# Constant first states for three scans in four: a selective scan whose carried states move to the first column, on one Trainium2 core

## The chip, the cores and the metric

The kernel runs on one core of a Trainium2 chip (trn2), as one launch. The metric is the device time of that launch in microseconds: the median of several executions of the same program. Beside it stands one profiled execution, from which every view of the trace is taken.

## The reference

Two layers follow each other on an input `x` of 4 images, 128 channels, 128 x 128 pixels, all fp32. The first is a selective state space model over the 16384 pixels of an image, taken as a sequence:

```
h1 = relu(xf @ mlp_w1.T + mlp_b1);  xm = h1 @ mlp_w2.T + mlp_b2
x_in, z = split(xm @ in_proj_w.T)
u = silu(causal_conv4(x_in) + conv_b)
dt, Bm, Cm = split(u @ x_proj_w.T)
delta = softplus(dt @ dt_proj_w.T + dt_proj_b);  A = -exp(A_log)
h = h * exp(delta * A) + delta * u * Bm      # per step: 256 channels x 16 states
y = sum over the states of h * Cm
out = ((y + u * D) * silu(z)) @ out_proj_w.T, group norm, silu, + x
```

The second layer weighs four spectral filters by a softmax of a pooled projection, and applies them in the Fourier domain. The change touches the line with `h` alone.

## The kernel before

The program has two blocks. `block0` is the first layer, up to about 6385 us of the span; `block1` is the second. Each engine runs its own queue in order.

`block0` cuts the sequence of an image into 32 **chunks** of 512 steps (`T`), so there are 128 chunks, counted `k`. The 256 channels x 16 states of a chunk are 4096 independent recurrences, 32 tiles of 128 partitions (32 channels x 4 states): a half `j` (2), a round `r` (4) and a place `p` (4). The function `place(r, p)` says which group of 32 channels stands at place `p` of round `r`. One `(j, r)` is a **unit** (8 in a chunk, unit 0 to unit 7), and its two pairs of places (0, 1 and 2, 3) are two **slots** `n`; a chunk is 16 slots (`NP`). What each engine does in a slot is an order written by hand: lists of (slot, phase, function), and within a slot the phases in the fixed order of the last loop of `block0`.

For one unit this happens:

- `dbu` (L370, GpSimd) makes du*B for places 1 to 3 in the tile `hb`, two slots ahead, from `rdu` and `rB`, which DMAs have spread over the partitions. For place 0 TensorE makes it in `b0` (L390), from `bt`.
- `exps` (L400, ScalarE) makes exp(delta*A) into `da`, one to three slots ahead. Places 1 to 3 lie in PSUM, one buffer each.
- `scans` (L419, VectorE) runs h = da*h + b along the 512 steps. Its first state `init` is 0 in the first chunk of an image; else it is one column of the tile `last` (shown as `st`), the last state of the same tile in chunk `k - 1`.
- h*C: for some places VectorE (L421), in place over `da`, for the others GpSimd (L426), from the tile `h`. `by_vector` says which: places 2 and 3 on VectorE, 0 and 1 on GpSimd as one instruction over two places, and some exceptions by the chunk's parity and by `norming(k)`. A chunk is norming when it is chunk 2 to 17 of image 1, 2 or 3, all counted from 0 (48 chunks: `k % 32` from 2 to 17); there the group norm of the image before runs beside the scans. The other 80 chunks are called plain here.
- The last state of each place is copied to `last` by ScalarE, one column after a VectorE product (L422), one or two columns after a GpSimd place (L561, in the next slot's phase `late`).
- `sums` (L440, TensorE) adds up h*C over the states.

Beside the scans, each chunk has its projections, convolution, SiLUs (L244, L247), softplus (L283) and `du` = delta*u on GpSimd (L319) for the next chunk, on slots that `pre` lists. ScalarE loads a table (`ACT_TABLE_LOAD`) when it goes from Exp to SiLU or softplus and back.

Of the kernel before, what the change touches and what calls it, by code (L numbers as in the profile page):

```python
# [26 lines left out]
F32 = mybir.dt.float32  # L27
AF = mybir.ActivationFunctionType
ALU = mybir.AluOpType
# [4 lines left out]
P = 128  # L34
T = 512
# [11 lines left out]
def kernel(ctx: ExitStack, tc: tile.TileContext, a: dict, out: bass.AP):  # L47
# [106 lines left out]
    spec = [dpool.tile([H, C, 2, WF], F32, tag=f"spec_{b}", name=f"spec_{b}") for b in range(EARLY)]  # L154
    shared = SimpleNamespace(**{k: v for k, v in locals().items() if k not in ("ctx", "tc")})
    block0(tc, shared)
    block1(tc, shared)


def block0(tc, s):  # L160
    nc, B, NCH, NH, NS, NG, ND, R, NX, KC, HALO, C, L, NF, DI = (
        s.nc, s.B, s.NCH, s.NH, s.NS, s.NG, s.ND, s.R, s.NX, s.KC, s.HALO, s.C, s.L, s.NF, s.DI,
    )
    NT, TH, HP = T // P, T // 2, P // 2
    with ExitStack() as ctx:
        def pool(name, bufs, **kw):
            return ctx.enter_context(tc.tile_pool(name=name, bufs=bufs, **kw))
# [4 lines left out]
        tiny = pool("tiny", 2)  # L172
# [13 lines left out]
        st = {}  # L186
        stats, outs = s.stats, s.outs

        def pre(k):
# [3 lines left out]
            b, i = divmod(k, NCH)  # L193
            d = st[k] = {}
# [127 lines left out]
            def rep_load(j):  # L322
# [9 lines left out]
                (NP - 2, "pe", z_mm), (NP - 1, "act", z_act), (NP + 2, "act", z_silu), (3, "pe", xd_mm), (4, "act", xd_act), (5, "pe", dt_mm), (5, "pe", xd_turn),  # L332
                (5 if k else 7, "act", bc_load), (6, "act", dt_act), (7, "act", xd_turn_act), (7, "pool", du_pool),
                (8, "pe", partial(du_turn, 0)), (9, "act", partial(rep_load, 0)),
                (8, "pool", partial(bt_act, 0, 0, 1)), (9, "act", partial(bt_act, 0, 1, 5)),
                (10, "act", partial(bt_act, 0, 5, 8)), (11, "pe", partial(du_turn, 1)),
                (11, "pool", partial(bt_act, 1, 0, 1)), (12, "act", partial(bt_act, 1, 1, 2)),
# [7 lines left out]
        def norming(k):  # L345

            return k >= NCH and 2 <= k % NCH < 2 + NCH // 2

        def place(r, p):


            return (p - r) % ND

        def by_vector(k, j, r, p):

            if norming(k):
                return p > 1 and (k % 2 == 1 or (j, r, p) != (1, 2, 2))
            return p > 1 or (k % 2 == 1 and (j, r, p) == (1, 2, 1))

        def dbu(u):  # L360

            k, r = divmod(u, NH * NG)
            j, r = divmod(r, NG)
            d = st[k]
            hb = d["hb", j, r] = hpool.tile([P, ND, T], F32, tag="hb", name=f"hb_{k}_{j}_{r}")
            p = 1
            while p < NG:
                m = place(r, p)
                n = min(NG - p, ND - m)
                nc.gpsimd.tensor_tensor(  # L370
                    hb[:, p : p + n, :], d["du", j][:, m : m + n, :], d["B"][:, p - 1 : p - 1 + n, :], ALU.mult
                )
                p += n

        def pair(n):

            k, r = divmod(n, NP)
            u, p = divmod(r, ND // 2)
            j, r = divmod(u, NG)
            return k, j, r, 2 * p  # L380

        def dbu_turn(n):

            k, j, r, p = pair(n)
            d = st[k]
            if p == 0:
                b = d["b0"] = psd.tile([P, T], F32, tag="b0", name=f"b0_{k}_{j}_{r}")
                for t in range(NT):
                    src = d["bt"][:, t, j * ND + place(r, 0), :, :].rearrange("p s d -> p (s d)")
                    nc.tensor.transpose(b[:, t * P : (t + 1) * P], src, s.ident)  # L390

        def exps(n, qs):

            k, j, r, p = pair(n)
            d = st[k]
            for q in qs:
                m = place(r, p + q)
                c = (j * NG + p + q) * ND + m
                da = (psd if p + q else p2).tile([P, T], F32, tag=f"da{p + q}", name=f"da{p + q}_{k}_{j}_{r}")
                nc.scalar.activation(da, d["delta", j][:, m, :], AF.Exp, scale=s.amat[:, c : c + 1])  # L400
                d["da", j, r, p + q] = da

        def scans(n):


            k, j, r, p = pair(n)
            d = st[k]
            hb = d["hb", j, r]
            das = [d.pop(("da", j, r, p + q)) for q in range(2)]
            dve = [q for q in range(2) if by_vector(k, j, r, p + q)]  # L410
            pool = [q for q in range(2) if q not in dve]
            last = d["last", j, r, p] = tiny.tile([P, 2], F32, tag=f"st{j}_{r}_{p}", name=f"st_{k}_{j}_{r}_{p}")
            if pool:
                h = p2.tile([P, 2, T], F32, tag="h", name=f"h_{k}_{j}_{r}_{p}", bufs=3)
            for q in range(2):
                b = hb[:, p + q, :] if p + q else d.pop("b0")
                init = 0.0 if k % NCH == 0 else st[k - 1]["last", j, r, p][:, q : q + 1]
                o = das[q] if q in dve else h[:, q, :]
                nc.vector.tensor_tensor_scan(o, das[q], b, init, ALU.mult, ALU.add)  # L419
            for q in dve:  # L420
                nc.vector.tensor_tensor(hb[:, p + q, :], das[q], d["C"][:, p + q, :], ALU.mult)  # L421
                nc.scalar.copy(last[:, q : q + 1], das[q][:, T - 1 : T])  # L422
            if pool:
                q = slice(pool[0], pool[-1] + 1)
                ps = slice(p + pool[0], p + pool[-1] + 1)
                nc.gpsimd.tensor_tensor(hb[:, ps, :], h[:, q, :], d["C"][:, ps, :], ALU.mult)  # L426
                todo[n + 1, "late"].append(partial(nc.scalar.copy, last[:, q], h[:, q, T - 1]))

        def sums(u):

# [81 lines left out]
        todo = defaultdict(list)  # L512
        for k in range(n_chunks):
            for at, phase, f in pre(k) + post(k):
                todo[at + (k - 1) * NP, phase].append(f)
# [30 lines left out]
        for n in range(n_chunks * NP):  # L546
            if n % 2 == 0:
                todo[n - 3, "early"].append(partial(exps, n, (0,)))
            todo[n - 1, "exps"].append(partial(exps, n, (1,) if n % 2 == 0 else (0, 1)))
            todo[n - 1, "turn"].append(partial(dbu_turn, n))  # L550
            todo[n, "scans"].append(partial(scans, n))
            if n % 2 == 0:
                todo[n - 2, "dbu"].append(partial(dbu, n // 2))
            else:
                todo[n + 2, "sums"].append(partial(sums, n // 2))
        slots = [n for n, _ in todo]
        with tc.manual_schedule():
            for n in range(min(slots), max(slots) + 1):
                for phase in ("turn", "sums", "pe", "exps", "late", "act", "pool", "dbu", "early", "gate", "scans", "dve", "end"):
                    for f in todo[n, phase]:  # L560
                        f()  # L561

# [509 lines left out]
```

## Time and profile before

| | |
|---|---|
| Median of 3 executions | 7099.01 us (7092.6 to 7100.89) |
| Profiled execution: time, span | 7100.83 us, 7099.1 us |
| Mean granted TensorE clock | 0.926 |
| Busy in the span | DVE (VectorE) 6843.7 us, POOL (GpSimd) 6807.6, ACT (ScalarE) 6144.4, PE (TensorE) 5656.9 |
| Scans (L419) | 4096, most 1.255 to 1.27 us each |
| h*C on VectorE, on GpSimd | 2064 instructions of one place; 984 of two places and 64 of one |

The profile is of one execution. A row of a group reads: line, engine, operation, tile written and tiles read, shapes, count, then busy time in us and mean ns of one, then the engine's idle time just before them and what ended it. A row of waits reads: who waited for whom, us in total, times, longest. A timeline row starts with its start in us and its length; equal neighbours are merged, and what stands in brackets is the engine's idle time before it. On VectorE, ScalarE and GpSimd an instruction starts some 0.04 to 0.1 us before the one ahead of it has ended, so the time that one takes from its engine is the distance of the starts, a little less than its length.

### The profile page before, as it was taken

How to read it: one execution, taken by the hardware profiler on the slowest of the kernel's cores; microseconds unless marked ns; L12 is line 12 of the kernel's file. 1: busy time of each engine (PE TensorE's matmuls, PEld its weight loads, DVE VectorE, ACT ScalarE, POOL GpSimd, SP SyncE). 2: the span in 40 equal slices, each digit the busy share in tenths (PEclk: the TensorE clock that was granted, in tenths of full speed). 3: DMA queues.
4: the chain of work that ended last, by engine and by line, in shares of the span. 5: the costliest groups of instructions: out<-in, count | busy, mean ns of one | idle time of the engine just before them, and what ended most of it. 6: DMA issues, size and time to landing. Idle time of an engine off the chain costs nothing.

```text
span 7099.1 us, 95554 instructions
## 1 busy us (share of the span) xinstructions
PE 5656.9 (80%) x28724; PEld 2700.3 (38%) x28724; DVE 6843.7 (96%) x7901; ACT 6144.4 (87%) x13836; POOL 6807.6 (96%) x3010
## 2 busy tenths in 40 slices
PE   6777777787777778787787778887778787877999
PEld 2333333333333333333333333333333333327888
DVE  6999999999999999999999999999999999997877
ACT  6888888888888888888989888898988989878886
POOL 6999999999999999999999999999999999997887
PEclk8988898888989989999999999999999999989999
DMA  6667667667787767777777777777878777768865
GB/s 141 160 153 164 159 149 165 160 150 175 179 196 181 188 169 167 181 181 179 192 193 196 189 174 177 174 184 172 200 188 200 191 170 178 169 143 293 273 218 190
DMA packets 759513, 1288.54 MB, mean 182 GB/s; under 512 B 81728, under 2 KB 192848, under 8 KB 758992
## 3 DMA queue, kind: packets, MB, share of 16 engines
q1 hardware_dynamic: 758848, 1282.16, 72.5%
q8 instruction: 226, 3.70, 0.2%
q14 instruction: 295, 2.42, 0.1%
q10 hardware_dynamic: 144, 0.26, 0.0%
HBM read 1025.52 MB, written 256.58 MB: 181 GB/s over the span
## 4 chain that ended last, share of the span: by engine, by line
ACT 30%; DVE 24%; POOL 18%; PE 10%; issue 10%; DMA 7%; SPq 1%; DVEq 0%; ACTq 0%; POOLq 0%
DVE da L419 12%; ACT da L400 12%; POOL hb L370 10%; POOL hb L426 7%; DVE h L419 7%; ACT L400 3%; DVE hb L421 3%; DMA rdelta<-dd 2%; ACT bt L313 2%; PE px L892 2%; DMA rdu<-dd 2%; ACT L247 2%; ACT L283 1%; ACT delta L283 1%; PE y L440 1%
## 5 line engine op out<-in xcount | busy, mean ns | idle before, releaser
L370 POOL TENSOR_TENSOR hb<-rdu,rB 128x1536 f32<-128x1536 f32 (+2 forms) x1536 | 3612.4, 2370 | 41.6 <-DMA rdelta<-dd 21.2
L400 ACT ACTIVATE da<-rdelta,amat 128x512 f32<-128x512 f32 x4096 | 2792.3, 699 | 123.3 <-DVE h L419 119.3
L426 POOL TENSOR_TENSOR hb<-h,rC 128x1024 f32<-128x1024 f32 (+1 forms) x1048 | 2411.1, 2302 | 89.3 <-DVE h L419 76.6
L419 DVE TENSOR_TENSOR_SCAN da<-da,st,hb 128x512 f32<-128x512 f32 x2000 | 2449.3, 1268 | 38.0 <-ACT da L400 27.1
L421 DVE TENSOR_TENSOR hb<-da,rC 128x512 f32<-128x512 f32 x2064 | 1309.7, 673 | 2.2
L419 DVE TENSOR_TENSOR_SCAN h<-da,st,b 128x512 f32<-128x512 f32 x992 | 1258.7, 1269 | 1.9 <-PE b L390 1.9
L440 PE MATMUL y<-hb,sel 128*32 128x512 f32 x8192 | 1243.4, 681 | 2.9 <-POOL hb L426 2.7
L419 DVE TENSOR_TENSOR_SCAN h<-da,st,hb 128x512 f32<-128x512 f32 x976 | 1223.1, 1255 | 1.4 <-ACT da L400 1.4
L390 PE MATMUL b<-ident,bt 128*128 128x128 f32 x4096 | 723.7, 298 | 448.9 <-DVE h L419 325.2
L239 PE MATMUL pp_cv<-xm,wck 128*128 128x512 f32 x2048 | 1013.7, 640 | 1.5 <-ACT xm L222 0.8
L313 ACT ACTIVATE bt<-pt_dut,xdt 128x256 f32<-128x256 f32 x2048 | 837.6, 473 | 181.1 <-PE pt_dut L302 180.9
L390 PEld LDWEIGHTS b<-ident,bt 128*128 128x128 f32 x4096 | 524.6, 151 | 943.2 <-DVE h L419 650.7
L422 ACT COPY st<-da 128x1 f32<-128x1 f32 x2064 | 267.9, 160 | 441.3 <-DVE hb L421 437.0
L239 PEld LDWEIGHTS pp_cv<-xm,wck 128*128 128x128 f32 x2048 | 396.0, 204 | 651.7 <-issue 420.8
L302 PE MATMUL pt_dut<-ident,du 128*128 128x128 f32 x1024 | 207.8, 337 | 407.2 <-POOL du L319 391.4
L850 POOL TENSOR_TENSOR wb<-wb,term 128x1040 f32<-128x1040 f32 x166 | 398.8, 2403 | 62.0 <-ACT term L840 56.6
L436 PE MATMUL y<-u,diag 128*128 128x512 f32 x512 | 303.3, 676 | 183.7 <-DVE zs L450 181.8
L277 PE MATMUL pp_dt<-xd,wdt 128*128 128x256 f32 x1024 | 299.2, 418 | 149.9 <-ACT pp_o L464 141.2
L302 PEld LDWEIGHTS pt_dut<-ident,du 128*128 128x128 f32 x1024 | 132.2, 165 | 652.6 <-POOL du L319 528.5
L400 ACT ACT_TABLE_LOAD x262 | 336.1, 1283 | 12.2 <-DMA rdelta<-dd 7.6
L319 POOL TENSOR_TENSOR du<-delta,u 128x1024 f32<-128x1024 f32 x128 | 301.1, 2353 | 29.4 <-ACT delta L283 27.9
L228 PE MATMUL pp_z<-xm,win 128*128 128x512 f32 x512 | 275.6, 636 | 59.5 <-ACT fq L504 53.7
(167 smaller groups left out, 8209.6 us busy)
## 6 DMA issues: line engine op xcount, KB each, us to landing
rdelta<-dd SPq DMA_DIRECT2D x1024, 256.0 KB, 4.8
rdu<-dd SPq DMA_DIRECT2D x1024, 256.0 KB, 7.8
rC<-bc SPq DMA_DIRECT2D x512, 256.0 KB, 7.4
rB<-bc SPq DMA_DIRECT2D x512, 192.0 KB, 4.6
dd<-delta SPq DMA_DIRECT2D x256, 256.0 KB, 7.7
dd<-du SPq DMA_DIRECT2D x128, 512.0 KB, 6.6
ft<-in_filt_w SPq DMA_DIRECT2D x108, 520.0 KB, 6.7
ob<-o SPq DMA_DIRECT2D x128, 256.0 KB, 2.1
```

Source lines behind the costliest of these rows:

```text
L239: nc.tensor.matmul(ps["cv", j], w, d["xm"][:, t : t + T], start=t == 0, stop=t == KC - 1)
L302: nc.tensor.transpose(ps["dut"][:, 2 * t + j, :], d["du"][:, j, at : at + P], s.ident)
L313: nc.scalar.activation(d["bt"][:, 2 * h + t, :, q, :], src, AF.Copy, scale=d["xdt"][:, 2 * h + t, R + q : R + q + 1])
L370: nc.gpsimd.tensor_tensor(hb[:, p : p + n, :], d["du", j][:, m : m + n, :], d["B"][:, p - 1 : p - 1 + n, :], ALU.mult)
L390: nc.tensor.transpose(b[:, t * P : (t + 1) * P], src, s.ident)
L400: nc.scalar.activation(da, d["delta", j][:, m, :], AF.Exp, scale=s.amat[:, c : c + 1])
L419: nc.vector.tensor_tensor_scan(o, das[q], b, init, ALU.mult, ALU.add)
L421: nc.vector.tensor_tensor(hb[:, p + q, :], das[q], d["C"][:, p + q, :], ALU.mult)
L426: nc.gpsimd.tensor_tensor(hb[:, ps, :], h[:, q, :], d["C"][:, ps, :], ALU.mult)
L436: nc.tensor.matmul(y, s.diag[:, j, :], d["u"][:, j, :], start=True, stop=False)
L440: nc.tensor.matmul(y[m * DG : (m + 1) * DG, :], s.sel, d["hb", j, r][:, p, :], start=False, stop=r == NG - 1)
L850: nc.gpsimd.tensor_tensor(wb, wb, u[n].terms[f], ALU.add)
```

## The change

A first state that is carried over only matters to the first step: h at step 0 is da at step 0 times the carried state, plus du*B at step 0. So for places 1 to 3 the product is added to the first column of du*B ahead of the scan, and the scan's first state is the constant 0. Place 0, whose du*B TensorE makes, keeps its state.

- `dbu` now writes columns 1 to 511 of places 1 to 3; column 0 is left to `first`.
- `first_products` (GpSimd, twice a chunk, one for each half `j`) makes du*B at step 0 for the 12 tiles of places 1 to 3 in one product of 12 columns, and delta*A at step 0 in another.
- `first_exp` (ScalarE) takes the Exp of the latter.
- `first_add` (GpSimd) multiplies it by the carried states, now one tile `last` for each half, and adds it to the former, 24 columns: the 12 are written twice, so that each round's three columns lie at a constant step. In the first chunk of an image there is a copy in place of this.
- `first` (ScalarE, once a unit, in a new phase of the slot before the unit's scans) copies the three columns to column 0 of `hb`.
- `by_vector`: in plain chunks place 1 of round 2 goes to VectorE in both halves and in every chunk (before: in the second half of odd chunks); in norming chunks place 1 of round 2 of the second half (before: none), and the even ones no longer give place 2 of that unit to GpSimd.

```diff
+                (12, "end", partial(first_products, k, 0)), (14, "late", partial(first_exp, k, 0)),
+                (14, "early", partial(first_add, k, 0)),
+                (20, "end", partial(first_products, k, 1)), (22, "late", partial(first_exp, k, 1)),
+                (22, "early", partial(first_add, k, 1)),
...
             if norming(k):
-                return p > 1 and (k % 2 == 1 or (j, r, p) != (1, 2, 2))
-            return p > 1 or (k % 2 == 1 and (j, r, p) == (1, 2, 1))
+                return p > 1 or (j, r, p) == (1, 2, 1)
+            return p > 1 or (r, p) == (2, 1)
...
-                    hb[:, p : p + n, :], d["du", j][:, m : m + n, :], d["B"][:, p - 1 : p - 1 + n, :], ALU.mult
+                    hb[:, p : p + n, 1:],
+                    d["du", j][:, m : m + n, 1:],
+                    d["B"][:, p - 1 : p - 1 + n, 1:],
+                    ALU.mult,
...
+        def first_products(k, j):
+            d = st[k]
+            du = d["du", j][:, :, 0:1].rearrange("p m o -> p o m")
+            b = d["B"][:, :, 0:1]
+            f = d["f", j] = tiny.tile([P, NG - 1, 1, ND], F32, tag=f"f{j}", name=f"f_{k}_{j}")
+            shape = [P, NG - 1, ND]
+            nc.gpsimd.tensor_tensor(f[:, :, 0, :], du.to_broadcast(shape), b.to_broadcast(shape), ALU.mult)
+            if k % NCH:
+                e = d["e", j] = tiny.tile(shape, F32, tag=f"e{j}", name=f"e_{k}_{j}")
+                a = s.amat.rearrange("p (j g m) -> p j g m", j=NH, m=ND)[:, j, 1:]
+                now = d["delta", j][:, :, 0:1].rearrange("p m o -> p o m")
+                nc.gpsimd.tensor_tensor(e, a, now.to_broadcast(shape), ALU.mult)
+
+        def first_exp(k, j):
+            if k % NCH:
+                nc.scalar.activation(st[k]["e", j], st[k]["e", j], AF.Exp)
+
+        def first_add(k, j):
+            shape = [P, NG - 1, 2, ND]
+            f = st[k]["f2", j] = tiny.tile(shape, F32, tag=f"g{j}", name=f"g_{k}_{j}")
+            b = st[k]["f", j].to_broadcast(shape)
+            if k % NCH:
+                e = st[k]["e", j]
+                nc.gpsimd.tensor_tensor(e, e, st[k - 1]["last", j][:, 1:], ALU.mult)
+                e = e.rearrange("p g (c m) -> p g c m", c=1)
+                nc.gpsimd.tensor_tensor(f, b, e.to_broadcast(shape), ALU.add)
+            else:
+                nc.gpsimd.tensor_copy(f, b)
+
+        def first(u):
+            k, r = divmod(u, NH * NG)
+            j, r = divmod(r, NG)
+            at, step = ND - r + 1, 2 * ND + 1
+            f = st[k]["f2", j].rearrange("p g c m -> p (g c m)")
+            nc.scalar.copy(st[k]["hb", j, r][:, 1:NG, 0], f[:, at : at + 2 * step + 1 : step])
...
-                init = 0.0 if k % NCH == 0 else st[k - 1]["last", j, r, p][:, q : q + 1]
+                m = place(r, 0)
+                init = 0.0 if p + q or k % NCH == 0 else st[k - 1]["last", j][:, 0, m : m + 1]
...
+                todo[n - 1, "first"].append(partial(first, n // 2))
...
-                for phase in ("turn", "sums", "pe", "exps", "late", "act", "pool", "dbu", "early", "gate", "scans", "dve", "end"):
+                for phase in ("turn", "sums", "pe", "exps", "late", "act", "pool", "dbu", "first", "early", "gate", "scans", "dve", "end"):
```

The copies to `last` (L422, L561) write to the columns of the new tile; their number changes only with `by_vector`.

More of the change, by code (lines that the diff above doesn't have):

```diff
@@ L411, in scans @@
             pool = [q for q in range(2) if q not in dve]
-            last = d["last", j, r, p] = tiny.tile([P, 2], F32, tag=f"st{j}_{r}_{p}", name=f"st_{k}_{j}_{r}_{p}")
+            if (j, r, p) == (j, 0, 0):
+                d["last", j] = tiny.tile([P, NG, ND], F32, tag=f"st{j}", name=f"st_{k}_{j}")
+            last = d["last", j].rearrange("p g m -> p (g m)")
+            at = [(p + q) * ND + place(r, p + q) for q in range(2)]
             if pool:
@@ L421, in scans @@
                 nc.vector.tensor_tensor(hb[:, p + q, :], das[q], d["C"][:, p + q, :], ALU.mult)
-                nc.scalar.copy(last[:, q : q + 1], das[q][:, T - 1 : T])
+                nc.scalar.copy(last[:, at[q] : at[q] + 1], das[q][:, T - 1 : T])
             if pool:
@@ L426, in scans @@
                 nc.gpsimd.tensor_tensor(hb[:, ps, :], h[:, q, :], d["C"][:, ps, :], ALU.mult)
-                todo[n + 1, "late"].append(partial(nc.scalar.copy, last[:, q], h[:, q, T - 1]))
+                a, b = at[pool[0]], at[pool[-1]]
+                to = last[:, a : b + 1 : max(b - a, 1)]
+                todo[n + 1, "late"].append(partial(nc.scalar.copy, to, h[:, q, T - 1]))
         def sums(u):
```

## The prediction

> **What bounds the kernel now.** I read the page's busy line first, then the groups kept apart by shape, then VectorE's waits, and last the timeline of one chunk.
>
> ```profile
> PE 5656.9 (80%) x28724; PEld 2700.3 (38%) x28724; DVE 6843.7 (96%) x7901; ACT 6144.4 (87%) x13836; POOL 6807.6 (96%) x3010
> ```
>
> VectorE (DVE) and GpSimd (POOL) are both full, ScalarE (ACT) is not far behind. The change touches the scan stage alone, 128 chunks that end at about 6385 us. There VectorE almost never waits:
>
> ```profile
> DVE da L419 <- ACT da L400: 27.1, 54, 3.0
> ...
> DVE da L419 <- POOL hb L370: 8.9, 12, 1.1
> ```
>
> So VectorE's work sets a chunk's time, except where ScalarE is late (54 waits). The prices, in the rows by shape:
>
> ```profile
> L419 DVE TENSOR_TENSOR_SCAN da<-da,st,hb 128x512 f32<-128x512 f32 x2000 | 2449.3, 1268 | 38.0 <-ACT da L400 27.1 <-POOL hb L370 8.9 <-issue 1.2
> ...
> L421 DVE TENSOR_TENSOR hb<-da,rC 128x512 f32<-128x512 f32 x2064 | 1309.7, 673 | 2.2
> ...
> L419 DVE TENSOR_TENSOR_SCAN h<-da,st,hb 128x512 f32<-128x512 f32 x976 | 1223.1, 1255 | 1.4 <-ACT da L400 1.4
> ...
> L370 POOL TENSOR_TENSOR hb<-rdu,rB 128x512 f32<-128x512 f32 x512 | 657.0, 1283 | 0.0
> ...
> L419 DVE TENSOR_TENSOR_SCAN da<-da,hb 128x512 f32<-128x512 f32 x64 | 74.5, 1210 | 1.1 <-issue 0.9
> ...
> L561 ACT COPY st<-h 128x2 f32<-128x2 f32 x984 | 183.6, 187 | 1.0 <-DVE h L419 1.0
> ```
>
> The x64 row is the first chunk of each image, where the first state already is the constant 0: 1210 against 1268 ns, and the h form 1197 against 1255. In the timeline the starts of following scans are 1.175 us apart with a state and 1.115 without. So a constant saves **60 ns a scan**.
>
> Where ScalarE is late: the norming chunks, 2 to 17 of images 1 to 3, all counted from 0. Chunk 40 opens at 2026.41 us. First the window from its unit 0's last product to unit 4's third scan, then VectorE's timeline at the window's end:
>
> ```profile
> 2032.40:2054.50 22.10, 13.38 (x67) 5.69 (x65) 21.86 (x25) 21.96 (x45) 22.10 (x11) 0.94 0.49 124
> ```
>
> ```profile
> 2053.01 1.25 DVE L419 TENSOR_TENSOR_SCAN h<-da,st,hb 128x512 f32<-128x512 f32 x1
> 2054.51 2.47 DVE L419 TENSOR_TENSOR_SCAN da<-da,st,hb 128x512 f32<-128x512 f32 x2 [0.25 <-ACT da L400]
> ```
>
> The columns after the length are PE, PEld, DVE, ACT, POOL. ScalarE works 21.96 of 22.10 us and never waits in it (four loads of its tables, both SiLUs, two norm activations, softplus), and at its end VectorE waits 0.25 us for it. This 22 us, in 48 of 128 chunks, is bound by ScalarE.
>
> **What the Trainium skill says.** "VectorE: DVE Perf Modes", section Scalar operands: a scalar is an instruction's constant or a [P, 1] operand read per partition. It gives no price for the latter; the trace does, 60 ns. "Perfetto Trace Analysis", Optimizing Scalar/DVE Operations: the write acknowledgement half of a small operation overlaps the next instruction. The trace agrees: L561 takes 187 ns, and the next start comes after 83. "ScalarE: Activation LUTs", Table sets: copies are in every table set. The trace agrees: L422 and L561 stand between Exps with no load. So the new copies load nothing, and the small Exps stand among Exps.
>
> **The change, part by part.** I count in starts, not durations.
>
> *VectorE.* 24 scans a chunk take a constant, in 124 chunks: 2976 x 0.060 = -178.6 us. Products on VectorE go from 2064 to 2256. Each moved one follows its own scan at once: in image 0, chunk 8 lasts 48.37 us and chunk 9, with one such product more, 49.11, so one costs 0.74 (two neighbouring products start 0.59 apart). Per chunk: plain even (40) gets two: 1.48 - 1.44 = +0.04, in the four first chunks +1.48; plain odd (40) one: -0.70; norming odd (24) one: -0.70; norming even (24) one and the third product of (1, 2) at 0.47 (0.59 less a wait for its own scan): -0.23. Sum: 1.4 + 5.9 - 28.0 - 16.8 - 5.5 = **-43 us**, if nothing else binds.
>
> *ScalarE.* 1024 `first` copies (128x3) and 248 Exps of 12 columns come in; by L561's step of 0.083 a copy is 0.085, an Exp I take at 0.10. From both sides: 0.04, the step between two adjacent L422, to 0.19, a whole L561. In plain chunks ScalarE waits for VectorE at unit 2's product and has 0.5 us in hand at unit 4, which covers -0.24 (four scans shorter) and -0.19; were it used up, 0.355 x 80 = 28 us would be open. 192 more one-column copies (L422) follow the moved products, 0.04 to 0.13 each, where ScalarE waits for VectorE anyway. In the norming stretch nothing covers them. Three copies and one Exp lengthen it by 3 x 0.085 + 0.10 = 0.355, and the ten scans in it that became shorter (three each in units 1 to 3, one in unit 4) only make VectorE wait longer: 0.60 lost. The wait at unit 4 grows from 0.25 to about 1.2 us. 48 x 0.955 = **+46 us**. So norming chunks go from 49.95 (odd) and 49.49 (even) to about 50.2 both.
>
> In the plain chunks of images 1 to 3 ScalarE comes late to unit 6 in 24 of 47: in 8 by 0.8 us, in the rest by little. There the second scan must now wait for `first` too, behind the heavy work of its slot: ten odd ones lose 0.4 to 0.8 each, the even ones, where the new product fills a wait that is there, 0.1: **+7 us**.
>
> *GpSimd.* Starts are 3.41, 2.32, 1.23 us apart for 1536, 1024, 512 columns: 0.145 us + 2.12 ns a column. "GPSIMD Engine Reference", Elementwise, has about 2.6 cycles an element with two inputs; 2.12 ns agrees. A plain chunk: 27.84 (L370) + 2.30 (L319) + 18.56 or 17.47 (L426, even or odd) = 48.7 or 47.6. After it: six pairs and two singles, 46.5, plus eight small operations; in norming chunks 47.6 plus eight. By the line, 12 columns are 0.17, 24 are 0.20: 6 x 0.17 + 2 x 0.20, and 0.1 for each of the two adds that wait for the product just before: 1.6 us a chunk. Its low end is that. High: the same page, Performance pitfalls, gives about 102 cycles for a read command that overlaps with none; for two inputs, an estimate of 0.17 us more each: 3.0 a chunk. Against 48.4 in plain chunks (VectorE's new time) 1.6 fits with 0.3 to spare; I take +4 us for uneven moments. Columns 1 to 511 instead of 512 save 0.05 a chunk; a penalty for the odd start is shown by no row. L916 writes rows of 65 columns at 1.25 us for 520, on the line, so broken rows cost nothing; I take 0.
>
> *Waits and queues.* No DMA is added or moved on SP's queue, and GpSimd issues none. `first_products` stand just before the L370 that already waits for the same rdu, at most 0.4 us earlier; that L370 waited 17 times for it, so 17 x 0.4 = 7 us of GpSimd's spare time at most. ScalarE's small Exp waits for them, and behind it in unit 4 stand the softplus and its loads: in chunk 40 the product before ends 1.8 us ahead of that place, so it is ready. GpSimd's second product waits for that Exp, with h*C queued behind: the Exp's place comes before the end of the L370 between them. `first` of round 0 waits for the add; it is late only at unit 0 of norming odd chunks, by about 1 us, where ScalarE has 2.5. TensorE: nothing changes.
>
> Sum: -43 + 46 + 7 + 4 = +14 on the profiled execution's 7100.8 us, which lies 1.8 above the median of 7099.0. **Forecast 7113 us.** About 0.2% (14 us) is what a measurement here can tell from no change, so this lies at the edge.
>
> **The rivals.**
> A, *faster*: ScalarE's stretch gives way, VectorE's saving counts everywhere: -43, 7056 us. For it: 96% VectorE, few waits. Against: the window above. It decides if the stretch has 0.9 us of slack a chunk in place of VectorE's existing 0.25 us wait.
> B, *GpSimd becomes the bound*: above 1.9 us of small operations in a plain chunk (0.21 each with the two waits). At 3.0: 1.1 x 76 plain chunks + 0.4 x 48 norming = about 103 us more, 7212; at 2.3, some 30 more, 7139. For it: 96% busy and no row for so small an operation. Against: the straight line.
> C, *the 60 ns belongs to first chunks and not to the constant*: then +135, about 7250 with ScalarE's additions. Against: all three scan forms differ by the same 58 to 61 ns, with the same operands otherwise.
>
> **How the numbers follow.** Forecast 0.62, split about evenly at the bound of +14 (ScalarE's small steps of 0.04 or 0.19 move it to +5 or +33); B 0.22; A 0.13; C 0.03. Faster: A and a little of the forecast's low end, if ScalarE's late places in plain chunks cost nothing, 0.17. Same: half of the forecast and some of B's mild end, 0.33. Slower: 0.50. The range runs from A's 7055 to 7165, the middle of B; C and B's high end are left out.
>
> **What would show it.** Right: constant scans at 1.20 us, in the same place of chunk 40 a wait of about 1.2 us of L472 (the scan's line there) for ScalarE, waits of DVE for ACT of some 50 us more in all, norming chunks of 50.2 and plain ones of 48.4; small GpSimd operations of 0.2 us and its idle time unchanged or larger. Wrong: VectorE's waits unchanged with a shorter span (A); GpSimd at 99% with waits of VectorE for L374 (B); scans still at 1.26 (C).

## The result, and the profile after

The changed kernel takes 7112.69 us (median of 10 runs, 7106.47 to 7117.54), the kernel before 7096.92 in the same comparison (10 runs, 7092.60 to 7102.64): a ratio of 1.0023, with a 95% interval of 1.0013 to 1.0032. So it is 16 us slower, 0.23%. Its profiled execution took 7110.89 us, with a span of 7109.1; that is 10 us over the profiled execution of before, because that one lay 4 us above its median and this one 2 us below.

The busy line of the changed kernel's page:

```profile
PE 5681.2 (80%) x28724; PEld 2716.6 (38%) x28724; DVE 6812.0 (96%) x8093; ACT 6288.1 (88%) x15276; POOL 6778.5 (95%) x3994
```

VectorE works 32 us less and GpSimd 29 us less than before, yet the span is longer; ScalarE works 144 us more. Two full engines became freer and the time went up, so the reader must look for a wait. The granted TensorE clock is 0.918 instead of 0.926, but it does not order the times: the fastest run below (7013.8 us) has 0.918 too. First the prices, from VectorE's and ScalarE's groups kept apart by shape:

```profile
L472 DVE TENSOR_TENSOR_SCAN da<-da,hb 128x512 f32<-128x512 f32 x2256 | 2638.5, 1211 | 40.9 <-ACT da L449 21.0 <-ACT hb L439 14.4 <-POOL hb L374 1.0
L474 DVE TENSOR_TENSOR hb<-da,rC 128x512 f32<-128x512 f32 x2256 | 1440.6, 676 | 7.2
...
L472 DVE TENSOR_TENSOR_SCAN h<-da,hb 128x512 f32<-128x512 f32 x816 | 979.1, 1200 | 47.1 <-ACT hb L439 47.0
```

```profile
L439 ACT COPY hb<-g 128x3 f32<-128x3 f32 x1024 | 206.3, 201 | 6.6 <-POOL g L430 4.0 <-POOL g L428 2.3
...
L416 ACT ACTIVATE e<-e 128x12 f32<-128x12 f32 x248 | 50.8, 205 | 0.0
```

Scans without a state operand take 1211 and 1200 ns, 57 and 55 less than the forms with one. But 82 us of idle time now stand ahead of them, put down to ScalarE, where it was 28.5. VectorE's waits name the instructions:

```profile
DVE h L472 <- ACT hb L439: 47.0, 58, 4.0
...
DVE da L472 <- ACT da L449: 21.0, 79, 1.8
...
DVE da L472 <- ACT hb L439: 14.4, 25, 1.1
```

L439 is the new copy of three first columns into hb. Where it is waited for, the timeline of the same norming chunk shows (chunk 40 opens at 2021.29 here; unit 4's second and third scan):

```profile
2048.24 1.23 DVE L472 TENSOR_TENSOR_SCAN h<-da,hb 128x512 f32<-128x512 f32 x1 [0.74 <-ACT hb L439]
2049.64 2.35 DVE L472 TENSOR_TENSOR_SCAN da<-da,hb 128x512 f32<-128x512 f32 x2 [0.17 <-ACT da L449]
```

and the windows of that stretch (unit 0's last product to unit 4's third scan) and of the whole chunk:

```profile
2027.10:2049.64 22.54, 15.19 (x73) 7.14 (x73) 21.48 (x25) 22.40 (x49) 22.46 (x15) 0.94 0.49 124
2021.29:2071.57 50.28, 38.51 (x159) 15.77 (x158) 49.18 (x57) 45.30 (x110) 49.53 (x30) 0.87 0.75 185
```

ScalarE works 22.40 of 22.54 us; it worked 21.96 of 22.10 before. The stretch is 0.44 longer although VectorE's scans in it are shorter. Adding up chunk lengths from the two traces, from one chunk's opening scan to the next:

| chunks | number | length before, mean | after | sum of the differences | foreseen |
|---|---|---|---|---|---|
| first of an image | 4 | 52.02 | 53.41 | +5.5 | +5.9 |
| image 0, even and odd | 31 | 48.37, 49.12 | 48.43, 48.43 | -10.0 | -10.6 |
| later plain, even and odd | 44 | 48.97, 49.60 | 49.08, 49.30 | -4.5 | -8 |
| norming, even | 24 | 49.54 | 50.45 | +21.8 | norming together +24 |
| norming, odd | 24 | 50.37 | 50.59 | +5.4 | |
| start and everything after chunk 126 | | | | -8.1 | 0 |

The prediction's further +4 us for uneven moments of GpSimd belongs to no one row. The last row cannot be put down to the change: across all the profiled runs of this case the start lies between 46.9 and 51.7 us and the end between 755 and 762, in no order that follows the edits. The rows above it sum to +18.1.

### The profile page after: what moved, and what is told of

It is laid out like the page before. It is cut to its first block, busy times and chain, and to the rows that moved or that the text cites. A ratio compares the mean times of both kernels' runs of the same rounds, so it can differ in the third digit from the quotient of the medians.

```text
span 7109.1 us, 98053 instructions
## 1 busy us (share of the span) xinstructions
PE 5681.2 (80%) x28724; PEld 2716.6 (38%) x28724; DVE 6812.0 (96%) x8093; ACT 6288.1 (88%) x15276; POOL 6778.5 (95%) x3994
## 4 chain that ended last, share of the span: by engine, by line
DVE 41%; ACT 17%; issue 12%; POOL 12%; PE 10%; DMA 7%; SPq 1%; DVEq 0%; ACTq 0%; POOLq 0%
DVE da L472 21%; DVE h L472 9%; DVE hb L474 8%; ACT da L449 7%; POOL hb L374 6%; POOL hb L479 4%; DMA rdelta<-dd 3%; PE px L948 2%; DVE zs L505 1%; PE pz L986 1%; ACT L449 1%; PE y L495 1%; DMA rdu<-dd 1%; POOL du L319 1%; PE po L998 1%
## 5 line engine op out<-in xcount | busy, mean ns | idle before, releaser
L374 POOL TENSOR_TENSOR hb<-rdu,rB 128x1533 f32<-128x1533 f32 (+2 forms) x1536 | 3601.7, 2361 | 0.2 <-POOL e L412 0.2
L472 DVE TENSOR_TENSOR_SCAN da<-da,hb 128x512 f32<-128x512 f32 x2256 | 2638.5, 1211 | 40.9 <-ACT da L449 21.0
L479 POOL TENSOR_TENSOR hb<-h,rC 128x1024 f32<-128x1024 f32 (+1 forms) x1024 | 2196.1, 2145 | 48.9 <-DVE h L472 46.1
L474 DVE TENSOR_TENSOR hb<-da,rC 128x512 f32<-128x512 f32 x2256 | 1440.6, 676 | 7.2
L495 PE MATMUL y<-hb,sel 128*32 128x512 f32 x8192 | 1264.0, 692 | 2.6 <-POOL hb L479 2.6
L472 DVE TENSOR_TENSOR_SCAN h<-da,hb 128x512 f32<-128x512 f32 x816 | 979.1, 1200 | 47.1 <-ACT hb L439 47.0
L313 ACT ACTIVATE bt<-pt_dut,xdt 128x256 f32<-128x256 f32 x2048 | 836.7, 472 | 127.3 <-PE pt_dut L302 127.1
L475 ACT COPY st<-da 128x1 f32<-128x1 f32 x2256 | 295.2, 161 | 369.6 <-DVE hb L474 360.9
L449 ACT ACT_TABLE_LOAD x262 | 336.1, 1283 | 11.9 <-DMA rdelta<-dd 7.2
L319 POOL TENSOR_TENSOR du<-delta,u 128x1024 f32<-128x1024 f32 x128 | 300.3, 2346 | 26.1 <-ACT delta L283 26.1
```

What stands on the lines that cost most here:

```text
L313: nc.scalar.activation(d["bt"][:, 2 * h + t, :, q, :], src, AF.Copy, scale=d["xdt"][:, 2 * h + t, R + q : R + q + 1])
L319: nc.gpsimd.tensor_tensor(du, d["delta"], d["u"], ALU.mult)
L374: nc.gpsimd.tensor_tensor(hb[:, p : p + n, 1:], d["du", j][:, m : m + n, 1:], d["B"][:, p - 1 : p - 1 + n, 1:], ALU.mult,)
L495: nc.tensor.matmul(y[m * DG : (m + 1) * DG, :], s.sel, d["hb", j, r][:, p, :], start=False, stop=r == NG - 1)
```

## The experiments

The theory on trial: VectorE's work sets the plain chunks and gains there; in the 48 norming chunks ScalarE's queue sets the first 22 us, so that VectorE's shorter scans only wait, and the copies and the small Exp come on top. Against it: ScalarE is short everywhere, or hides all; GpSimd's small products are what costs. All ratios are to the kernel before on the same chip. Its median lay between 7095.9 and 7099.6 in the five comparisons, so kernels of different comparisons are best set side by side by their ratios; where the text subtracts medians of two comparisons and the ratios say otherwise, both are given.

| run | median us | ratio | 95% interval |
|---|---|---|---|
| the change | 7112.7 | 1.0023 | 1.0013 to 1.0032 |
| the change, Squares late | 7070.6 | 0.9959 | 0.9946 to 0.9971 |
| before, Squares late | 7080.0 | 0.9971 | 0.9959 to 0.9982 |
| the change, no carry | 7074.6 | 0.9966 | 0.9952 to 0.9980 |
| before with ScalarE's additions | 7123.6 | 1.0035 | 1.0022 to 1.0047 |
| no carry, products at their old places | 7013.8 | 0.9883 | 0.9870 to 0.9897 |
| the change, small products doubled | 7176.3 | 1.0114 | 1.0100 to 1.0128 |
| the change in plain chunks only | 7089.6 | 0.9989 | 0.9983 to 0.9996 |
| Squares late, early turn | 7088.6 | 0.9988 | 0.9981 to 0.9994 |
| Squares late, a quarter of the products back | 7051.5 | 0.9937 | 0.9923 to 0.9950 |
| Squares late, bt late | 7042.2 | 0.9925 | 0.9912 to 0.9937 |
| all three of these | 7033.5 | 0.9913 | 0.9900 to 0.9927 |
| before, Squares late, bt late | 7061.4 | 0.9951 | 0.9938 to 0.9965 |

### Taking work out of ScalarE's stretch

```
-(at[2] + sums, "act" if sums else "end", partial(norm_stats, i)),
+(at[2] + (8 if sums and i < NCH - 2 else sums), "act" if sums else "end", partial(norm_stats, i)),
```

> The changed kernel with one thing moved: ScalarE's two Squares of the norm (128x512 each), which stand at slot 4 of a norming chunk, inside the stretch of 22 us before unit 4, stand at slot 11, behind it (not for the last two of an image). Theory (ScalarE sets that stretch, and VectorE's 0.60 us of saving there are spent waiting): the wait of 1.07 us a norming chunk goes, norming chunks fall from 50.5 to about 49.4, 48 x 1.07 = 50 us less than the changed kernel, about 7062, which is 0.995 of the kernel before. Rival 1 (ScalarE is short over the whole chunk, so the Squares are paid wherever they stand): no change, about 7113, and the wait turns up behind slot 11. Rival 2 (GpSimd with its small products sets the norming chunks): no change, and VectorE waits for GpSimd instead.

Measured: 7070.6 us, 42 less than the changed kernel (45 by the ratios), and below the kernel before too. The same scans of chunk 40 in its timeline, and its windows of the stretch and of the chunk:

```profile
2041.81 1.20 DVE L472 TENSOR_TENSOR_SCAN h<-da,hb 128x512 f32<-128x512 f32 x1
2042.92 2.35 DVE L472 TENSOR_TENSOR_SCAN da<-da,hb 128x512 f32<-128x512 f32 x2
```

```profile
2021.49:2042.92 21.43, 14.00 (x68) 5.96 (x66) 21.28 (x25) 21.20 (x45) 21.35 (x14) 0.95 0.52 132
2015.68:2064.86 49.18, 37.56 (x159) 15.30 (x158) 48.99 (x57) 45.06 (x110) 49.02 (x30) 0.88 0.74 188
```

The brackets after both scans are gone, and the chunk is 49.2 instead of 50.3. ScalarE works as much in the chunk as before the move (45.06 against 45.30): not its total is short but its share of these 22 us, which excludes the first rival. VectorE and GpSimd now work 48.99 and 49.02 of 49.18 us, so both are close to being the bound.

Why 45 and not the expected 50: the norming chunks gave 45 us in this trace. Chunk 17 of each image, whose Squares stayed, keeps a wait of 0.8 us at unit 4 and gained nothing, so 45 chunks of 48 could gain; they gained 1.0 each. The wait of 0.15 us at unit 2, which the expectation counted in its 1.07, stayed in every norming chunk.

> The kernel before with the same move of the two Squares from slot 4 to slot 11 of a norming chunk. Theory: only its wait of 0.25 us in 48 chunks can go, 12 us, about 7085 (0.998). Rival 1 (ScalarE short over the whole chunk): no change or slower. If this gained as much as the move does in the changed kernel (50 us), the wait there would not be the change's doing.

Measured with the same line changed in the kernel before: 7080.0, 20 us less against 12 expected and 42 to 45 in the changed kernel. Most of the wait was thus made by the change. The norming chunks gave 17.6 us in its trace (means of 49.20 and 49.98).

### ScalarE's additions by themselves

The changed kernel without `first_products`, `first_exp`, `first_add` and `first`, and with all 512 columns of du*B:

```
-                todo[n - 1, "first"].append(partial(first, n // 2))
...
-                    hb[:, p : p + n, 1:],
+                    hb[:, p : p + n, :],
```

> The changed kernel without what carries the state: no first columns, so no small GpSimd products, no 3-column copies and no small Exps on ScalarE, and du*B is made over all 512 columns; the scans of places 1 to 3 start from 0 in every chunk, so the state of the chunk before is left out there. VectorE's work is that of the changed kernel. Theory: what goes is the additions alone, 48 x 0.355 = 17 us in the norming chunks, 5 to 9 in the late plain chunks, 4 in the first chunks: about 28 us less than the changed kernel, 7085 (0.998 of before), the wait at unit 4 about 0.7 us instead of 1.07. Rival B (GpSimd's 1.64 us of small products a chunk are on the path): up to 128 x 1.64 = 210 us less, about 6900. Rival A (the additions are hidden): no change, 7113.

Measured: 7074.6, 38 us less than the changed kernel (41 by the ratios) against 28 expected. In the norming chunks the sum fell by 21.5, in the late plain ones by 17.3; in the first chunks nothing (+1.1). Chunk 40's timeline still has the wait, but smaller:

```profile
2045.71 1.22 DVE L468 TENSOR_TENSOR_SCAN h<-da,hb 128x512 f32<-128x512 f32 x1 [0.19 <-ACT da L445]
2047.34 2.35 DVE L468 TENSOR_TENSOR_SCAN da<-da,hb 128x512 f32<-128x512 f32 x2 [0.41 <-ACT da L445]
```

0.60 us of idle time remain where no copy is left. They are not yet the other half of the theory, the saving that the stretch swallows, for 0.25 of them stood there in the kernel before. The lengths show that half: a norming chunk of this run takes 49.86 us in the median, even and odd. Had VectorE's saving counted in full, it would take 49.26 and 49.25 by the prediction's prices (49.49 - 0.23 and 49.95 - 0.70). So 0.60 us a chunk are swallowed.

The reverse, the kernel before with 1024 copies and 248 Exps onto scratch:

```
+            nc.scalar.copy(tiny.tile([P, 3], F32, tag="z3", name=f"z3_{u}"), s.amat[:, 0:3])
...
+                nc.scalar.activation(tiny.tile([P, 12], F32, tag="z12", name=f"z12_{k}_{j}"), s.amat[:, 0:12], AF.Exp)
```

> The kernel before with ScalarE's additions alone, at the same places in its order: 1024 copies of 3 columns and 248 Exps of 12 columns, onto scratch that nobody reads. VectorE and GpSimd as before. Theory: 0.355 us more in the stretch of 48 norming chunks, 17 us, and up to 9 us in the late plain chunks: 7114 to 7123 (1.0025 to 1.0037). Rival (ScalarE hides them): no change, 7097. Rival (ScalarE is short everywhere): 1024 x 0.086 + 248 x 0.102 = 113 us, 7210.

Measured: 7123.6, 24 us more than the 7099.6 of that comparison. The norming chunks gave 21.5 of it, the late plain ones 5.4, image 0 nothing (48.37 and 49.12 to a hundredth). So the norming chunks change by 21.5 us whether all the additions are taken out of the one kernel or ScalarE's alone are put into the other, and "short everywhere" (113 us) falls. In the late plain chunks the two runs differ, 17.3 against 5.4: there the copies alone are not the whole, and what is taken out with them is GpSimd's work and the wait of hb for its first columns. How the 12 us split between these two was not separated.

### What GpSimd's small products cost

> The changed kernel with four more GpSimd products of 12 columns per half (scratch, read by nobody), eight a chunk beside its eight. Each takes 0.17 to 0.29 us, so 1.4 to 2.3 us more a chunk. GpSimd's idle time in the changed kernel is 0.41 us in chunks of image 0, 0.9 in late plain chunks, 1.1 to 1.3 in norming chunks. Theory (GpSimd's spare time covered the change's own products and is nearly used up): the excess is paid, about 0.95 x 31 + 0.45 x 44 + 0.2 x 48 = 60 us at the low price, 7170, up to 7285 at the high one. Rival (GpSimd is far from deciding): no change, 7113. Rival B (GpSimd decides already): all of it, 128 x 1.4 = 180 us or more, 7290.

```
+                for x in range(4):
+                    z = tiny.tile([P, 12], F32, tag="z", name=f"z{x}_{k}_{j}", bufs=3)
+                    nc.gpsimd.tensor_tensor(z, s.amat[:, 0:12], s.amat[:, 12:24], ALU.mult)
```

Measured: 7176.3, 64 us more than the changed kernel, the low end of the theory. GpSimd was close to its limit and not at it. The group of the added products, and that of ScalarE's copies:

```profile
L431 POOL TENSOR_TENSOR z<-amat 128x12 f32<-128x12 f32 x992 | 177.2, 210 | 0.0
```

```profile
L442 ACT COPY hb<-g 128x3 f32<-128x3 f32 x1024 | 203.9, 199 | 43.0 <-POOL g L428 38.1 <-POOL g L433 4.4
```

VectorE's waits in this run again name the copy (88.2 us for L442), as in the changed kernel. Those at unit 4 of the norming chunks are the same 0.91 us as there. New ones stand at unit 5: 0.7 us in a chunk of image 0, where the changed kernel has none. It is tempting to explain them by the 43.0 us for which the copies waited for GpSimd. But nearly all of that idle time stands ahead of unit 0's copies, where VectorE hardly ever waits, and unit 5's copies have none. The timeline of chunk 19, which opens at 1003.67 us, shows the way:

```profile
1029.41 2.34 POOL L319 TENSOR_TENSOR du<-delta,u 128x1024 f32<-128x1024 f32 x1
...
1031.80 1.12 PE L302 MATMUL pt_dut<-ident,du 128*128 128x128 f32 x4 [6.66 <-POOL du L319]
...
1032.95 0.48 ACT L313 ACTIVATE bt<-pt_dut,xdt 128x256 f32<-128x256 f32 x1 [2.20 <-PE pt_dut L302]
...
1035.46 0.22 ACT L442 COPY hb<-g 128x3 f32<-128x3 f32 x1
...
1035.77 1.22 DVE L475 TENSOR_TENSOR_SCAN h<-da,hb 128x512 f32<-128x512 f32 x1 [0.69 <-ACT hb L442]
```

GpSimd comes to its du product (L319) 25.7 us after the opening instead of 23.3 (medians of image 0 here and in the changed kernel), TensorE's turn of du waits for it, ScalarE waits 2.20 us for TensorE, and the copy, seven instructions further down ScalarE's queue, is late without having waited itself. So a VectorE wait that names ScalarE is here GpSimd's lateness, passed on by two engines.

### The constant alone

The run without the carry, with `by_vector` as in the kernel before:

```
-                return p > 1 or (j, r, p) == (1, 2, 1)
-            return p > 1 or (r, p) == (2, 1)
+                return p > 1 and (k % 2 == 1 or (j, r, p) != (1, 2, 2))
+            return p > 1 or (k % 2 == 1 and (j, r, p) == (1, 2, 1))
```

> The constant 0 alone: no first columns and no small products (the state of the chunk before is left out at places 1 to 3, as in the run without the carry), and the h*C products stand where the kernel before has them. VectorE has 60 ns less a scan, GpSimd has its full load of before. Theory: in plain chunks VectorE would need 46.9 and 47.7 us against 48.4 and 49.1 before, but GpSimd's work, which 1.9 us of idle a chunk covered in the run without carry and with 192 products fewer, now sets the pace at about 48 us; norming chunks stay bound by ScalarE's stretch at about 49.9. So only a part of the 179 us shows: 30 to 60 us less than before, 7040 to 7070 (0.991 to 0.996). Rival (VectorE alone sets the time): up to 179 us less, 6920. Rival C (the 60 ns are not those of the state operand): no change, 7097.

Measured: 7013.8, 83 us less than before, beyond the expected 30 to 60. GpSimd has no gap left above 60 ns in the median chunk of any kind: it is the bound, as expected, but the norming chunks take 49.6 on average (48.79 and 50.34), not 49.9, and those of image 0 48.0. Together with the two runs above this splits the change, each difference taken from the ratios times 7097: the constant -83 us, the products moved to VectorE +59, the carry +40, in all +16. The +59 is what the move costs when there is no small work on GpSimd to make room for.

### Plain chunks alone

> The change in the plain chunks alone; the 48 norming chunks do what the kernel before does (state as first state, du*B over 512 columns, its h*C places, no copies). Theory (plain chunks gain, norming chunks lose): the norming chunks' 27 us come back, plain and first chunks, start and end keep what the changed kernel's trace has (17 us less than before): 7080 (0.9975). Rival A (the change gains in norming chunks too): slower than the changed kernel, above 7113. Rival (GpSimd's products cost in the plain chunks): no faster than before, 7097.

```
+                m = place(r, p + q)
+                carried = p + q == 0 or norming(k)
+                init = st[k - 1]["last", j][:, p + q, m : m + 1] if carried and k % NCH else 0.0
```

(with `first` and its three companions left out, and the old places of h*C, where `norming(k)`.) Measured: 7089.6, a ratio of 0.9989. The norming chunks are back at 49.59 and 50.42, and the run is faster than the changed kernel and than the kernel before: the first is what rival A excluded, the second what the rival on GpSimd excluded. The 17 us of the expectation held 8 of start and end that are not the change's; the plain and first chunks alone gave 9 in this trace and 7 in the medians.

### Late plain chunks: three attempts and their sum

In the late plain chunks a wait of VectorE at unit 6 was left. In the changed kernel's ScalarE waits:

```profile
ACT bt L313 <- PE pt_dut L302: 127.1, 111, 3.2
```

(180.9 in the kernel before.) With the Squares late, chunk 54 has ScalarE idle from 36.0 to 38.0 us after its opening, then L313, and behind it unit 6's copy L439 at 38.4 and the Exps.

```
-(11, "pe", partial(du_turn, 1)),
+(11, "turn", partial(du_turn, 1)),
```

> The changed kernel with the late Squares, and one more step moved: TensorE's second turn of du (four transposes, slot 11) stands ahead of the y sums of that slot instead of behind them. In late plain chunks ScalarE stood idle 1.3 to 2.0 us before its first bt product of that turn, with unit 6's 3-column copy and Exps queued behind it, and VectorE then waited 0.45 to 0.61 us at unit 6 in 20 of 33 of these chunks. Theory (that wait is ScalarE's queue standing behind TensorE's): the wait goes, 44 x 0.3 = 13 us less than with the late Squares alone, 7058 (0.994). Rival (ScalarE has too much work there): no change, 7071.

Measured: 7088.6, 18 us slower than with the late Squares alone (21 by the ratios) instead of 13 faster. ScalarE's waits of this run:

```profile
ACT xm L222 <- PE pp_xm L214: 100.6, 50, 3.0
...
ACT bt L313 <- PE pt_dut L302: 29.7, 47, 3.0
```

With the late Squares alone the second was 121.5. TensorE's turn came earlier (in chunk 54 the copy stands at 36.3 instead of 38.4), but what followed on TensorE came later: pp_xm started at 39.7 instead of 37.8, and ScalarE stood before it from 39.0 to 41.7. The stall changed its name and grew, and VectorE now waited at unit 7, in 39 of the 44 late plain chunks.

```
-(11, "pool", partial(bt_act, 1, 0, 1)), (12, "act", partial(bt_act, 1, 1, 2)),
+(12, "act", partial(bt_act, 1, 0, 2)),
```

> The changed kernel with the late Squares, and ScalarE's first bt product of the second turn (slot 11) put behind unit 6's 3-column copy and the first Exp of slot 12, to the rest of its group; TensorE's order is untouched, where the run with the early turn only handed the stall on to xm. Theory (unit 6 waits because those two stand behind a ScalarE that waits for TensorE's turn): VectorE's wait of 0.45 to 0.61 us at unit 6 goes in the late plain chunks, 44 x 0.3 = 13 us less than with the late Squares alone, 7058. Rival (ScalarE loses the time it stands anyway, and what follows is late instead: xm, the Exps of slot 13): no change, 7071.

Measured: 7042.2, 28 us less than with the late Squares alone (24 by the ratios), about twice what was expected. Its ScalarE waits:

```profile
ACT bt L313 <- PE pt_dut L302: 40.8, 48, 3.0
...
ACT xm L222 <- PE pp_xm L214: 7.4, 9, 3.2
```

The instruction that waits now stands behind those that are ready. The late plain chunks gave 24 us in the trace; none of the 33 in the middle of their stretches (chunks 19 to 29 of images 1 to 3) has a VectorE wait above 0.1 us.

```
-            return p > 1 or (r, p) == (2, 1)
+            return p > 1 or ((r, p) == (2, 1) and (j == 0 or k % 4 != 3))
```

> The changed kernel with the late Squares, and in every fourth plain chunk (20 chunks) the h*C product of half 1, round 2, place 1 goes back from VectorE to GpSimd. VectorE saves 0.70 us in such a chunk; GpSimd has 1.27 us more there, against 0.41 us of idle time a chunk in image 0 and 0.9 later, so 1.6 to 3.6 us over four chunks. Theory (the slack of the buffers carries GpSimd's lag over to the next three chunks): 20 x 0.70 = 14 us less than with the late Squares alone, 7057. Rival (the lag is waited for in the same chunk): 1.27 - 0.41 - 0.70 = 0.16 us more or nothing, 7071 to 7074.

Measured: 7051.5, 19 us less than with the late Squares alone (16 by the ratios). In the trace 15 us of it lie in late plain chunks, where the wait at unit 6 shrank as well, so image 0 is the cleaner test. There a chunk with the product back takes 47.68 us instead of 48.44, but the chunk behind it 48.89 in the mean: in four of seven VectorE waits 0.24 to 0.68 us at unit 5, again behind a late L319 and L313. The lag is carried over by one chunk and then in part waited for: image 0 gained 3.1 us, where eight products of 0.70 would give 5.6.

> The changed kernel with the three edits that helped together: the late Squares, the late bt product, and every fourth plain chunk's product back on GpSimd. The late bt gained 28 us beyond the late Squares, the quarter 19, of which 15 lay in the late plain chunks, where the late bt has already taken the wait. Theory (GpSimd's lag is carried over, so VectorE's 0.70 us in 20 chunks still come on top): 7042 - 14 = 7028. Rival (the quarter's gain in the late plain chunks was that same wait): only image 0's 3 us and no more, 7039.

Measured: 7033.5, a ratio of 0.9913, 9 us below the late bt alone and so between theory (14) and rival (3): image 0 gives 3.4, the late plain chunks 4.3. Of the runs that carry the states it is the fastest, 62 us under the kernel before.

> The kernel before with the late Squares and the late bt product. It asks what the change is worth once ScalarE's queue no longer stands in its way. With the late Squares alone this kernel took 7080; its wait at unit 6 was 0.42 us in 11 of 15 even late plain chunks. Theory (the change is then worth VectorE's saving in odd chunks, plain and norming, less what GpSimd sets in the norming chunks): 21 x 0.42 x 0.7 = 6 us less, 7074, so the change gives 32 us against 7042. Rival (the late bt helps both alike): 7080 - 28 = 7052, and the change is worth 10 us as with the late Squares alone.

Measured: 7061.4, between the theory's 7074 and the rival's 7052. With both of ScalarE's steps out of the way the change is worth 0.9951 - 0.9925 = 0.0026, some 18 us; with the late Squares alone 0.0012, 9 us, where the two intervals overlap.

## Why the prediction was right

Forecast 7113, measured 7112.7; its +14 came as +16. That the two agree to 0.3 us is luck: the median that it started from lay 2.1 us above the later one, norming and late plain chunks each cost 3 to 4 us more than foreseen, the +4 for GpSimd's uneven moments did not show in image 0, and start and end of the two profiled executions differ by 8 us. The mechanism is what held. By its steps:

- **VectorE's price.** 60 ns a scan, and 0.74 a moved product. The plain chunks of image 0, where nothing else interferes, went to 48.43 both, as summed. In norming chunks the prediction's sums leave 49.0 for VectorE's work (49.95 - 0.70 less the wait of 0.25); the late Squares, which take the wait at unit 4 away, show 48.99.
- **ScalarE's additions.** A copy was taken at 0.085; in the changed kernel the step from a copy to the next Exp is 0.086 in the median, and from the 12-column Exp 0.102 where bt follows (0.10 was taken), but 0.215 where the softplus's table load follows, as it does in the stretch. Neither loads a table. Foreseen in the norming chunks 0.355 x 48 = 17 us, measured 21.5 in either direction: 4 too low. How much of the 4 is that step before the load was not separated.
- **The swallowed saving.** 0.60 was foreseen, and 0.60 is what the lengths show when the copies go. In all the wait at unit 4 was to rise from 0.25 to 1.2; it is 0.91, and 1.07 with 0.15 at unit 2 that was not foreseen. The idle time understates the loss, since a scan that waits also loses its overlap with the one before: chunk 40's second and third scan of unit 4 start 1.40 us apart with 0.17 of idle time, and 1.11 without. Norming chunks: foreseen 50.2, measured 50.27 and 50.28 in the median.
- **Late plain chunks.** A loss of 7 us was foreseen at unit 6, which left a gain of 8 in the 44 chunks; the gain was 4.5. The place was right: of the 33 chunks named above 8 of 15 even ones wait there by 0.83 in the mean and 11 of 18 odd ones by 0.38. "Behind the heavy work of its slot" was the wrong reason: ScalarE stood idle there, waiting for TensorE's turn, as the run with the late bt shows.
- **GpSimd.** 1.6 us a chunk was foreseen. By starts the four operations of a half are 0.170, 0.173, 0.291 and 0.187 us, 0.82 a half and 1.64 a chunk; the 0.291 holds 0.08 of idle time, since the add reads the product just before it. The groups by shape:

```profile
L374 POOL TENSOR_TENSOR hb<-rdu,rB 128x511 f32<-128x511 f32 x512 | 653.7, 1277 | 0.0
...
L428 POOL TENSOR_TENSOR g<-f,e 128x24 f32<-128x24 f32 x248 | 56.6, 228 | 19.4
L407 POOL TENSOR_TENSOR f<-rdu,rB 128x12 f32<-128x12 f32 x256 | 55.6, 217 | 69.7 <-DMA rdu<-dd 39.7 <-DMA xr<-in_x 15.1 <-issue 10.4
...
L426 POOL TENSOR_TENSOR e<-e,st 128x12 f32<-128x12 f32 x248 | 53.8, 217 | 39.9 <-ACT e L416 39.2
```

  The odd start at column 1 costs nothing (1277 against 1283 ns), and the 102 cycles for a read command in "GPSIMD Engine Reference", Performance pitfalls, from which the prediction's high price was worked out, do not show in the strided or broadcast operands: 0.170 us is what the prediction's straight line gives for 12 columns. The spare of 0.3 us a plain chunk was 0.41 by image 0's gaps; with the products doubled, image 0's chunks grew by 1.0 us for 1.4 of work, so it is hardly more.
- **Waits.** That GpSimd's second product finds its Exp ready was wrong: L426 waited 39.2 us for L416. And L407 waited 39.7 for rdu, one time of 20.4 among them. Both are waits that moved, into GpSimd's spare time: ahead of du*B its idle time fell from 41.6 to 0.2 us and ahead of the paired h*C from 89.3 to 48.9. Its idle time in the span rose from 291 to 331 us, and the VectorE waits that name it nearly vanished (8.9 to 1.0 ahead of the da scans).
- **The rivals.** A (the stretch gives way) falls by the window of 22.40 in 22.54. B (GpSimd becomes the bound) falls for this kernel, but by half a microsecond a chunk, as the doubled products and the late Squares show. C (no saving by the constant) falls by the scans of 1.20.

## What to carry to other kernels

A saving on the busiest engine counts only in stretches where nobody else ends last; find these stretches first, price the saving there at zero, and price at full whatever the change adds to the engine that does bind. On an in-order engine a short instruction that waits for another engine should stand behind the ready ones: moving one such product of 0.47 us by one slot gave 24 us here by the ratios, more than the change gained with the late Squares (9) or with both moves (18). When a wait names an instruction, go back along that engine's queue to the last instruction that waited, and see for whom, before calling the engine slow.

## What the runs showed of the hardware that was not expected

- A 12-column GpSimd product takes 0.17 us from start to start even with strided and broadcast operands, so the eight small operations of a chunk cost 1.6 us. One that reads the result of the one just before it takes 0.29.
- A VectorE product that follows its own scan starts 35 ns after the scan's recorded end, where following scans overlap by 80 ns: the dependence costs 0.12 us, which is most of why a moved product costs 0.74 and not 0.59.
- A recorded wait for a ScalarE copy of the same form was ScalarE's own work in one place (unit 4 of the norming chunks: 22.40 us busy of 22.54) and GpSimd's lateness in another (unit 5 with the products doubled), where the copy itself had waited for nothing and ScalarE had stood for 2.20 us seven instructions earlier.
